# A conditioned residual layer: the order annealed anew, row totals and SBUF low parts on GpSimd, W in two halves

## The chip, the cores and the metric

One NeuronCore of a Trainium2 chip runs the kernel. The metric is the device time of one execution in microseconds, as the median of several runs. The engines are TensorE (PE in the profile, PEld for its weight loads), VectorE (DVE), ScalarE (ACT), GpSimd (POOL) and SyncE (SP, which issues most of the DMAs). Each engine works through its own list of instructions in order, and they wait for each other by semaphores.

## The reference

x is (4, 1024, 512), cond (4, 256), W (1536, 512), b (512), all fp32.

```python
hidden = jnp.concatenate([cond, cond], axis=-1)
x_mean = jnp.mean(x, axis=1, keepdims=True)
fused = jnp.concatenate([x, x_mean * ones_L, hidden[:, None, :] * ones_L], axis=-1)
out = x + jax.nn.relu(jnp.einsum('bld,do->blo', fused, W) + b)
```

So there is one large product, x times the first 512 rows of W, and one bias vector for each of the four rows of the batch: mean(x) times the next 512 rows of W, plus cond times the sum of the last two blocks of 256 rows, plus b.

## The kernel before

The 4096 positions of x are 32 output tiles of 128 positions by 512 columns, eight for each row of the batch. The product is made with fp32r operands split into a high and a low part, hi and lo of x and of W, as hi·hi + lo·hi + hi·lo. With four blocks j of 128 along the 512 summed columns, a tile takes 12 products of 128x128 by 128x512, into one of five PSUM banks (bank t mod 5 for tile t). The last tile is made in two half widths.

x is read twice. Once it comes as z, in rows of 512 bytes, so that a 32x32 block transpose on DVE gives the stationary operand. z comes in ten units (UNITS): tiles 0, 1, 2 to 3, 4 to 7, and then four tiles each; a unit has four transfers `Zu.i` into one of three buffers. The second time it comes as plain x (`Xg.h`, two tiles each) for the residual, into the slot from which the result is stored.

All work is cut into named tasks, and the string ORDER lists them; the loop at the end of the kernel issues them one after the other, so each engine's list is the order of its tasks in the string. A name ends in @d, @a or @p where the engine is chosen there: DVE, ACT or POOL. The tasks:

- `Zu.i`, `Wp.i`, `Mi`, `V`, `C`, `B`, `Xg.h`, `St`: the DMAs of z, of W's first block, of the mean's block, of the condition's block, of cond, of b, of x, and the stores. All are on SP's queue but W0, which is on ACT's. A transfer has one of eight semaphores and is issued when the earlier one with that semaphore has landed.
- `whj`, `wlj` (lines 207, 205, 211): high and low part of W, block j. `fill` (L129): a product of zeros in bf16 that keeps PE going before data is there.
- `Tu.j`, `hu.j`, `lu.j` (L229, L235, L241): for block j of unit u the transpose on DVE, the high part on ACT, which also sums it along the positions into `sums`, and the low part. Of the units of four tiles, the transposes of blocks 0 and 2 go to PSUM (px), those of 1 and 3 to SBUF (xT). GpSimd has no access to PSUM.
- `pt.j.n` (L339): one product; `pt.j`: all three.
- The bias of row r: `ac`, `t`, `g`, `d` make the condition's part, `prr` and `tor.j` (L274 to L281) the means from `sums`, `as` puts the condition's part into a PSUM bank, `mr.j` (L293) adds the mean's four blocks on DVE, `f`, `fa` fold the upper half of the partitions onto the lower, `vh`, `vl` split the result, `pbr` (L317) sums over the partitions and broadcasts with a matmul by ones, and `bc` copies the bias to SBUF. These steps wait for each other, from `to` to `bc`.
- A tile's end, by WAYS. Tiles 0 to 11 (K) are copied out of the bank by ACT before the bias is there (`K`), then `b` on POOL adds the bias (L410), `r` on ACT takes the relu and `F` on POOL adds x (L422). Tiles 12 to 17 (B) are copied with the bias added by DVE (`K`, L414), then `r` and `F` alike. Tiles 18 to 31 (I) get the bias into the bank ahead of the products (`P`, ACT, L393), and `F` on DVE takes relu and sum in one (L397). A bank is free again when `K` or `F` has read it.

Of the kernel before, what the change touches and what calls it, by code (L numbers as in the profile page):

```python
# [18 lines left out]


ORDER = """
W0.0@a W0.2@a W0.1@a W0.3@a Z1.0 Z1.2 Z1.1 Z1.3 Z0.0 Z0.2 Z0.1 Z0.3 W1.0 W1.2 W1.1 W1.3 T1.2 T1.0 T1.1 h1.0
wh0r@d h1.1 l1.0@d wh0l@d l1.1@p Z2.0 Z2.2 Z2.1 Z2.3 T0.1 fill fill fill fill fill fill fill fill fill p1.0.0
T0.0 p1.0.1 h0.1 wl0l@d h0.0 l0.1@d wl0r@d l0.0@p T1.3 p1.0.2 T0.2 h1.3 p0.0.1 W2.0 W2.2 W2.1 W2.3 wh2@d h0.2
p0.0.2 h1.2 p0.0.0 l0.2@p wh1@d p1.2.0 l1.3@p T0.3 wl2@d p1.1.0 h0.3 l1.2@p p0.2.1 p1.1.1 Z3.0 Z3.2 Z3.1 Z3.3
wl1@d p0.2.2 p1.2.2 l0.3@d p0.1.0 p1.1.2 T2.0 p0.1.1 T2.3 p0.1.2 h2.0 T2.2 p1.2.1 B p0.2.0 wh3@a l2.0@d C T2.1
h2.3 p3.0 V wl3@d h2.1 Z4.0 Z4.2 Z4.1 Z4.3 p1.3.0 l2.3@d h2.2 p0.3.0 l2.1@d p0.3.2 pr0 p2.0 l2.2@d M0 M2 M1 M3
p1.3.2 p3.1 p1.3.1 p3.2 K1@a Z5.0 Z5.2 Z5.1 Z5.3 p2.3 T3.1 p0.3.1 T3.0 p2.2 h3.1 p3.3 h3.0 l3.1@d K0@a p2.1
l3.0@d T3.2 p6.1 ac0@p K2@a to0.0 T3.3 p4.0 h3.2 Z6.0 Z6.2 Z6.1 Z6.3 ac1@p h3.3 p7.0 l3.3@d p4.1 t2 t1 p6.0
l3.2@d p7.1 to0.1 t3 t0 g0.0 p4.3 g0.1 d0.0 T4.1 p5.3 T4.0 h4.1 p5.1 T4.2 d0.1 h4.0 p4.2 to0.3 h4.2 l4.0@d  # L30
p5.2 K4@a l4.1@p to0.2 T4.3 p5.0 as0 l4.2@d Z7.0 Z7.2 Z7.1 Z7.3 p6.2 K5@a m0.0 p7.3 g1.0 m0.1 K3@a p6.3 X1.0
d1.0 m0.2 X0.0 g1.1 p7.2 X3.1 h4.3 m0.3 X0.1 p10.0 d1.1 g2.0 l4.3@d p9.2 f0 pr1 d2.0 p9.0 K6@a fa0 g2.1 p9.1
T5.1 K7@a d2.1 T5.3 p10.1 vh0 p8.1 h5.1 vl0 h5.3 p9.3 l5.1@p T5.2 T5.0 p10.2 h5.2 l5.3@p Z8.0 Z8.2 Z8.1 Z8.3
p11.3 h5.0 l5.2@d to1.2 pb0 to1.0 p11.0 l5.0@d bc0@a X4.1 to1.3 p10.3 to1.1 as1 b1@p p11.1 m1.0 K10@a p11.2
K9@a b2@p T6.0 g3.1 T6.1 p8.0 m1.1 h6.1 p15.3 T6.3 r2 l6.1@p p14.3 m1.2 r1 p15.1 K11@a m1.3 b0@p h6.3 p8.3
T6.2 f1 p8.2 l6.3@d Z9.0 Z9.2 Z9.1 Z9.3 b4@p h6.0 p12.1 fa1 T7.1 p12.2 vh1 b3@p l6.0@d h7.1 p12.3 vl1 h6.2
p15.2 F1 T7.3 K8@a p16.1 T7.0 h7.3 l6.2@d b5@p pb1 p16.0 bc1@a pr2 l7.1@d p14.2 h7.0 F2 T7.2 as2 p13.1 to2.0
to2.1 h7.2 m2.0 p13.2 r4 to2.2 p12.0 m2.1 r0 F4 p15.0 to2.3 m2.2 p13.0 F0 m2.3 p14.0 l7.0@d f2 p13.3 l7.3@p
g3.0 S0 fa2 X5.1 p16.3 K12@d vh2 d3.0 p14.1 r3 vl2 p16.2 r12 K14@d b7@p p17.0 K13@d r14 pb2 l7.2@d p17.3 F3
bc2@a T8.0 p17.2 P18 T8.2 P19 p17.1 T8.3 S3 r5 X5.0 T8.1 p18.3 S2 h8.2 F5 X3.0 p18.1 h8.0 l8.2@d X4.0 p18.2  # L40
X2.1 r13 K16@d d3.1 h8.3 p19.2 K15@d h8.1 p19.0 K17@d P21 l8.1@p l8.0@d p18.0 X6.1 as3 pr3 S1 T9.0 p21.2 P20
X2.0 l8.3@p T9.1 h9.0 S4 p21.0 T9.2 r7 p21.3 to3.0 F14 F18 P22 p19.1 h9.2 T9.3 p20.0 h9.1 to3.2 b6@p P23 p19.3
to3.1 m3.0 h9.3 b11@p p22.2 m3.1 p22.0 m3.2 b8@p p23.0 to3.3 m3.3 p20.3 f3 p20.1 r16 fa3 p22.1 F16 l9.2@d vh3
p20.2 r15 vl3 p22.3 b10@p F19 p23.1 F22 S19 pb3 l9.1@p p23.3 X1.1 l9.3@d bc3@a S5 p23.2 r17 F20 S22 b9@p P24
S16 p21.1 S20 P27 p24.1 X6.0 r11 F21 p27.1 F11 l9.0@d P26 p27.2 F23 r6 p27.3 P25 F6 p27.0 p25.2 F7 F27 p26.0
S27 P31r F12 r9 p24.2 S7 S6 P28 p31.2r S11 p31.1r F9 p31.0r p24.3 p26.1 F13 S9 X7.0 p26.2 S18 F15 S12 p25.1
X7.1 p24.0 S13 F17 p26.3 F24 p25.0 F26 S24 P29 p28.1 S26 p25.3 p28.0 F25 p29.0 S25 P30 p28.3 S15 r8 S21 p29.3
P31l F8 S17 r10 p31.1l p28.2 F10 S8 p31.3r S14 F28 p30.3 F31r p30.1 S28 S31r p30.2 S10 p30.0 p29.2 F30 p29.1
S30 p31.3l S23 F29 p31.0l p31.2l S29 F31l S31l
""".split()  # L50


# [1 line left out]
def kernel(  # L54
# [81 lines left out]
    def task(name):  # L136
        def put(f):
            assert name not in tasks, name
            tasks[name] = f
        return put  # L140

    def dma(e, **kw):
        (nc.scalar if e == "a" else nc.sync).dma_start(**kw)  # L143
# [115 lines left out]
    for r in range(B):  # L259
        for k in range(KH):  # L260
            @task(f"g{r}.{k}")
            def _(e, r=r, k=k):
# [8 lines left out]
        @task(f"pr{r}")
        def _(e, r=r, n_early=n_early):
            if n_early > 1:
                nc.vector.tensor_reduce(tot[:, r], sums[:, r, :, :n_early], AX.X, ALU.add)  # L274
# [1 line left out]
            nc.vector.tensor_scalar(pre[:, r], src, 1.0 / L, None, ALU.mult)

        for j in range(J):
            @task(f"to{r}.{j}")
            def _(e, r=r, j=j, n_early=n_early):  # L280
                nc.vector.scalar_tensor_tensor(  # L281
                    tot[:, r, j : j + 1], sums[:, r, j, n_early : n_early + 1], 1.0 / L, pre[:, r, j : j + 1],
                    ALU.mult, ALU.add,
                )
# [4 lines left out]

        for j in range(J):  # L290
            @task(f"m{r}.{j}")
            def _(e, r=r, j=j):
                nc.vector.scalar_tensor_tensor(  # L293
                    acc, w_mean[:, j, :], tot[:, r, j : j + 1], acc, ALU.mult, ALU.add
                )
# [16 lines left out]
        def _(e, low=low, high=high):
            nc.vector.tensor_tensor(v_acc[high], acc[low], v_acc[low].bitcast(F32), ALU.subtract)  # L313

        @task(f"pb{r}")
        def _(e):
            nc.tensor.matmul(acc, lhsT=ones, rhs=v_acc, start=True, stop=True)  # L317

        @task(f"bc{r}")
        def _(e, r=r):  # L320
            nc.scalar.activation(biases[r], acc, AF.Copy)  # L321
# [139 lines left out]
```

## Time and profile before

| | us |
|---|---|
| median of three runs | 113.5 |
| lowest, highest | 112.43, 113.69 |
| the profiled execution | 113.67 |
| its span, first to last instruction | 111.9 |

The page gives, for one execution, the busy time of each engine, then the span in 40 slices, DMA queues, the chain of work that ended last, and groups of like instructions. Three further views of the trace are used: busy time of the engines in chosen stretches (the columns are the stretch, its length, then busy us and instructions of PE, PEld, DVE, ACT and POOL, the granted clock, the DMA share and GB/s), the list of waits (who waited for whom: us in total, times, longest), and the time line (start, length, engine, line, operation, and in brackets how long the engine stood idle before it and for whom).

### The profile page before, as it was taken

How to read it: one execution, taken by the hardware profiler on the slowest of the kernel's cores; microseconds unless marked ns; L12 is line 12 of the kernel's file. 1: busy time of each engine (PE TensorE's matmuls, PEld its weight loads, DVE VectorE, ACT ScalarE, POOL GpSimd, SP SyncE). 2: the span in 40 equal slices, each digit the busy share in tenths (PEclk: the TensorE clock that was granted, in tenths of full speed). 3: DMA queues.
4: the chain of work that ended last, by engine and by line, in shares of the span. 5: the costliest groups of instructions: out<-in, count | busy, mean ns of one | idle time of the engine just before them, and what ended most of it. 6: DMA issues, size and time to landing. Idle time of an engine off the chain costs nothing.

```text
span 111.9 us, 1435 instructions
## 1 busy us (share of the span) xinstructions
PE 97.5 (87%) x409; PEld 75.9 (68%) x409; DVE 81.2 (73%) x150; ACT 61.5 (55%) x152; POOL 65.6 (59%) x59
## 2 busy tenths in 40 slices
...
GB/s 86 172 190 239 217 230 346 212 227 259 242 226 230 227 230 244 373 287 191 244 196 196 205 117 247 408 348 403 75 3 204 405 390 316 282 406 402 405 403 77
DMA packets 27698, 28.41 MB, mean 254 GB/s; under 512 B 1701, under 2 KB 18345, under 8 KB 27690
## 3 DMA queue, kind: packets, MB, share of 16 engines
...
## 4 chain that ended last, share of the span: by engine, by line
PE 34%; DVE 34%; ACT 8%; issue 6%; DMA 6%; SPq 4%; POOL 3%; DVEq 0%; ACTq 0%
PE po L339 34%; DVE acc L293 10%; DVE lo L241 5%; DVE xT L229 5%; DVE tot L281 4%; DVE px L229 4%; SPq L143 4%; DMA out_dram<-x 3%; ACT hi L235 3%; ACT term L263 2%; DMA z<-in_x_dram 2%; DVE v_acc L313 2%; DVE acc L305 2%; ACT fold L301 2%; POOL cond L267 1%
## 5 line engine op out<-in xcount | busy, mean ns | idle before, releaser
L339 PE MATMUL po<-w_hi,hi 128*128 128x512 f32 (+1 forms) x132 | 51.4, 395 | 4.1 <-DVE o L414 2.1
L339 PE MATMUL po<-w_lo,hi 128*128 128x512 f32 (+1 forms) x132 | 51.7, 395 | 1.1 <-DVE w_lo L211 1.1
L339 PE MATMUL po<-w_hi,lo 128*128 128x512 f32 (+1 forms) x132 | 51.4, 391 | 0.0
L339 PEld LDWEIGHTS po<-w_hi,hi 128*128 128x128 f32 x132 | 25.3, 192 | 11.7 <-ACT hi L235 2.6
L339 PEld LDWEIGHTS po<-w_lo,hi 128*128 128x128 f32 x132 | 25.6, 194 | 6.6 <-DVE w_lo L211 1.5
L422 POOL TENSOR_TENSOR x<-o,x 128x512 f32<-128x512 f32 x18 | 22.9, 1290 | 10.1 <-ACT o L418 9.4
L339 PEld LDWEIGHTS po<-w_hi,lo 128*128 128x128 f32 x132 | 25.5, 193 | 4.8
L397 DVE SCALAR_TENSOR_TENSOR x<-po,x 128x512 f32<-128x512 f32 x13 | 8.8, 686 | 13.9 <-PE po L339 13.9
L241 POOL TENSOR_TENSOR lo<-xT,hi 128x512 fp32r<-128x512 f32 (+1 forms) x13 | 13.0, 1011 | 9.6 <-ACT hi L235 9.6
L410 POOL TENSOR_TENSOR o<-o,bias 128x512 f32<-128x512 f32 x12 | 16.2, 1366 | 0.4 <-ACT bias L321 0.4
L235 ACT ACTIVATE hi<-xT 128x512 fp32r<-128x512 f32 (+2 forms) x24 | 12.0, 499 | 7.9 <-DVE xT L229 7.8
L229 DVE STREAM_TRANSPOSE xT<-z 128x512 f32<-128x512 f32 (+2 forms) x24 | 12.2, 529 | 5.6 <-DMA z<-in_x_dram 5.6
L293 DVE SCALAR_TENSOR_TENSOR acc<-w_mean,tot,acc 128x512 f32<-128x512 f32 x16 | 11.9, 747 | 0.4
L393 ACT ACTIVATE po<-bias 128x512 f32<-128x512 f32 x13 | 7.6, 593 | 8.1 <-DVE x L397 8.1
L235 ACT ACTIVATE hi<-px 128x512 fp32r<-128x512 f32 (+1 forms) x16 | 9.0, 563 | 4.4 <-DVE px L229 2.5
L418 ACT ACTIVATE o<-o 128x512 f32<-128x512 f32 x18 | 10.9, 620 | 0.4 <-DVE o L414 0.4
L241 DVE TENSOR_TENSOR lo<-xT,hi 128x512 fp32r<-128x512 f32 (+2 forms) x11 | 9.4, 851 | 2.3 <-ACT hi L235 2.3
L241 DVE TENSOR_TENSOR lo<-px,hi 128x512 fp32r<-128x512 f32 (+1 forms) x16 | 10.3, 641 | 0.6 <-ACT hi L235 0.6
L229 DVE STREAM_TRANSPOSE px<-z 128x512 f32<-128x512 f32 (+1 forms) x16 | 10.4, 667 | 0.0
L406 ACT ACTIVATE o<-po 128x512 f32<-128x512 f32 x12 | 7.0, 588 | 5.0 <-PE po L339 4.9
L257 POOL TENSOR_TENSOR wc<-x 128x512 f32<-128x512 f32 x2 | 2.5, 1282 | 11.6 <-DMA x<-in_L_cond_W_dram 11.6
L267 POOL TENSOR_TENSOR cond<-b_sb,term 128x512 f32<-128x512 f32 x4 | 5.6, 1402 | 4.1 <-ACT term L263 4.1
...
## 6 DMA issues: line engine op xcount, KB each, us to landing
...
```

Source lines behind the costliest of these rows:

```text
L229: nc.vector.transpose(xT.rearrange("p (n t) -> p n t", t=Q), zs[u % Z_BUFS][:, : n * NQ, j * Q : (j + 1) * Q])
L235: nc.scalar.activation(his[buf][:, col : col + m], xT, AF.Copy, accum_out=sums[:, r, j, s : s + 1])
L241: nc_of[e].tensor_tensor(los[buf][:, col : col + m], xT, his[buf][:, col : col + m].bitcast(F32), ALU.subtract)
L267: nc.gpsimd.tensor_tensor(conds[r % 2], conds[r % 2] if k else b_sb, terms[k], ALU.add)
L293: nc.vector.scalar_tensor_tensor(acc, w_mean[:, j, :], tot[:, r, j : j + 1], acc, ALU.mult, ALU.add)
L339: nc.tensor.matmul(v, lhsT=a[:, col : col + P], rhs=m, start=WAYS[t] != "I" and key not in done, stop=done.count(key) == 3 * J - 1, skip_g ...
L393: nc.scalar.activation(bank(t), biases[r], AF.Copy)
L397: nc.vector.scalar_tensor_tensor(x_tile(t), bank(t), 0.0, x_tile(t), ALU.max, ALU.add)
L406: nc.scalar.activation(o, bank(t), AF.Copy)
L410: nc_of[e].tensor_tensor(o, o, biases[r], ALU.add)
L418: nc.scalar.activation(o, o, AF.Relu)
L422: nc.gpsimd.tensor_tensor(x_tile(t), o, x_tile(t), ALU.add)
```

## The change

- ORDER is a new list. Its tasks are those of before but for the points below.
- `l0.1`, `l0.3`, `l3.1`, `l3.3`, `l4.3`, `l6.3`, `l7.1` and `l9.3` go from DVE to POOL and `l1.1` from POOL to DVE, so that from unit 3 on all low parts of SBUF pieces are on POOL and all those of PSUM pieces on DVE.
- `pr` and the four `to` of a row on DVE become one `to` on POOL: two instructions of 128x4 for rows 1 to 3, three for row 0.
- W's first block comes in two groups of four transfers, of two blocks each, and no longer in three groups of one, two and one blocks. `wh0r` and `wh1` are on ACT, `wh3` on DVE.
- There are 11 `fill` in place of 9.
- Eight matmuls stand at the end of the kernel, into the bank `acc`, which nothing reads after them, with 128, 96 or 66 columns of the stationary operand, from column 0 or 1.

The new list is given here up to `pb3` and for its last lines.

```diff
@@ ORDER @@
...
+W0.0@a W0.2@a W0.1@a W0.3@a Z0.0 Z0.2 Z0.1 Z0.3 Z1.0 Z1.2 Z1.1 Z1.3 wh0l@d wh0r@a wh1@a W1.0 W1.2 W1.1 W1.3
+wl0r@d wl0l@d T0.0 T0.1 h0.0 wl1@d h0.1 l0.0@p fill fill fill fill fill fill fill fill fill fill fill p0.0.0
+p0.0.2 Z2.0 Z2.2 Z2.1 Z2.3 p0.1.0 T1.0 l0.1@p T1.1 p0.1.2 h1.0 T0.2 p0.0.1 T0.3 h1.1 p0.1.1 T1.3 p1.0.0 h0.3
+l1.0@d p1.0.2 l1.1@d h1.3 l0.3@p p1.1.0 Z3.0 Z3.2 Z3.1 Z3.3 wh3@d h0.2 p1.0.1 p1.1.2 wh2@d l0.2@p p0.3.1 T1.2
+p0.3.0 wl3@d l1.3@p p0.2.0 h1.2 p0.2.1 l1.2@p p1.3.0 wl2@d p1.3.2 C p1.2.0 T2.2 V p1.1.1 p0.2.2 T2.0 h2.2 B
+p1.2.1 p1.3.1 h2.0 Z4.0 Z4.2 Z4.1 Z4.3 l2.2@d p1.2.2 p0.3.2 T2.3 p2.2 l2.0@d h2.3 p2.0 l2.3@d T2.1 p2.3 h2.1
+l2.1@d p3.0 Z5.0 Z5.2 Z5.1 Z5.3 p3.1 T3.3 p2.1 T3.2 h3.3 t2 p3.2 T3.0 h3.2 l3.3@p p3.3 K1@a l3.2@d h3.0 t3
+ac0@p t1 p6.2 T3.1 K2@a l3.0@d p4.2 M0 M2 M1 M3 h3.1 t0 p4.3 l3.1@p g0.0 p6.0 K0@a K3@a p6.3 ac1@p p6.1 d0.0
+g0.1 p7.0 T4.3 Z6.0 Z6.2 Z6.1 Z6.3 p4.0 T4.1 h4.3 p4.1 T4.0 K6@a l4.3@p T4.2 h4.1 p5.3 h4.2 p7.3 l4.1@p h4.0
+p7.1 K4@a l4.0@d d0.1 p8.3 g1.0 T5.1 p5.2 Z7.0 Z7.2 Z7.1 Z7.3 l4.2@d to0 as0 p5.0 d1.0 T5.3 h5.1 p11.3 T5.2
+p5.1 T5.0 l5.1@p p8.2 h5.0 m0.0 p8.1 g1.1 X5.0 m0.1 g2.0 p9.0 d1.1 Z8.0 Z8.2 Z8.1 Z8.3 m0.2 h5.3 p11.0 h5.2
+m0.3 l5.3@p p9.3 K5@a l5.0@d p11.2 f0 d2.0 g2.1 p8.0 fa0 p9.2 l5.2@d K8@a d2.1 T6.1 p7.2 vh0 p10.1 vl0 X0.0
+K7@a T6.2 p13.3 h6.1 X0.1 T6.3 p10.3 l6.1@p T6.0 pb0 X1.0 p9.1 bc0@a to1 p10.0 as1 b2@p X4.0 K9@a p11.1 m1.0
+g3.0 p13.0 b0@p m1.1 Z9.0 Z9.2 Z9.1 Z9.3 h6.3 p10.2 m1.2 g3.1 b1@p p14.0 h6.0 m1.3 p12.0 l6.0@d f1 l6.3@p
+p12.1 T7.1 K10@a p12.3 K11@a fa1 b5@p p14.1 T7.0 vh1 X4.1 h7.1 p12.2 vl1 b3@p h6.2 p15.0 T7.3 h7.0 l6.2@d pb1
+l7.1@p p14.2 h7.3 T7.2 p16.3 bc1@a l7.0@d h7.2 p13.2 T8.0 as2 to2 p16.2 l7.3@p r0 m2.0 p15.1 r1 m2.1 r2 F0
+p14.3 m2.2 p15.3 F1 m2.3 p15.2 K12@d f2 p13.1 d3.0 S1 fa2 p16.0 X5.1 T8.1 S0 vh2 p17.2 b4@p X3.0 h8.0 vl2
+p17.1 r5 l8.0@d pb2 F2 p16.1 K13@d bc2@a p17.3 T8.3 P18 F5 p17.0 K14@d r3 h8.1 l7.2@d p18.3 P19 K17@d l8.1@p
+p18.2 T8.2 P22 p18.0 T9.0 F3 h8.2 p19.1 r12 l8.2@d p22.3 h9.0 d3.1 T9.1 p22.1 h8.3 T9.2 p18.1 r4 K15@d l8.3@p
+h9.1 p22.2 F18 P20 p19.0 F4 T9.3 P23 p19.3 h9.2 p20.1 S4 K16@d h9.3 S18 p23.1 as3 to3 X2.0 b6@p P21 S2 p23.0
+m3.0 S3 p19.2 m3.1 X2.1 b10@p r6 X3.1 p21.3 m3.2 S5 p20.3 X1.1 l9.3@p m3.3 p23.2 l9.2@d f3 p20.2 b7@p fa3
+p22.0 F19 vh3 b9@p p20.0 vl3 p21.1 F20 F12 pb3 F22 p21.2 S20 bc3@a X6.1 l9.0@d p21.0 b8@p P27 r7 p23.3 P24
...
+P29 S24 p28.2 r15 S17 S11 p30.3 F14 S23 p29.2 S16 F15 p28.0 S14 p30.0 F28 F13 p31.3l S28 p30.2 S31r p29.0 S15
+F30 p29.3 S30 p29.1 S13 p31.0l F29 p31.1l p31.2l S29 F31l S31l
 
 
@@ -104,7 +103,7 @@
     cT = sb("cT", [P, KH, Q])
     sums = sb("sums", [P, B, J, 4])
     tot = sb("tot", [P, B, J])
-    pre = sb("pre", [P, B, J])
+    pre = sb("pre", [P, J, 2])
     one = sb("one", [P, 1])
 
     ps_o = [banks.tile([P, D], F32, name=f"po{i}") for i in range(O_BANKS)]
@@ -163,7 +162,7 @@
             @task(f"Z{u}.{i}")
             def _(e, z=z, r=r, i=i, k0=k0, n=n):
                 dma(e, out=z[i * Q : (i + 1) * Q, : n * NQ], in_=zv[r, i, :, k0 * NQ : (k0 + n) * NQ, :])
-    for part, (j0, n) in enumerate([(0, 1), (1, 2), (3, 1)]):
+    for part, (j0, n) in enumerate([(0, 2), (2, 2)]):
         for i in range(NQ):
             @task(f"W{part}.{i}")
             def _(e, i=i, j0=j0, n=n):
@@ -266,22 +265,14 @@
             def _(e, r=r, k=k):
                 nc.gpsimd.tensor_tensor(conds[r % 2], conds[r % 2] if k else b_sb, terms[k], ALU.add)
 
-        n_early = len(row_units[r]) - 1
-
-        @task(f"pr{r}")
-        def _(e, r=r, n_early=n_early):
-            if n_early > 1:
-                nc.vector.tensor_reduce(tot[:, r], sums[:, r, :, :n_early], AX.X, ALU.add)
-            src = tot[:, r] if n_early > 1 else sums[:, r, :, 0]
-            nc.vector.tensor_scalar(pre[:, r], src, 1.0 / L, None, ALU.mult)
-
-        for j in range(J):
-            @task(f"to{r}.{j}")
-            def _(e, r=r, j=j, n_early=n_early):
-                nc.vector.scalar_tensor_tensor(
-                    tot[:, r, j : j + 1], sums[:, r, j, n_early : n_early + 1], 1.0 / L, pre[:, r, j : j + 1],
-                    ALU.mult, ALU.add,
-                )
+        @task(f"to{r}")
+        def _(e, r=r, n=len(row_units[r])):
+            add, v = nc.gpsimd.tensor_tensor, sums[:, r]
+            if n == 4:
+                add(pre, v[:, :, :2], v[:, :, 2:], ALU.add)
+                v = pre
+            add(tot[:, r], v[:, :, 0], v[:, :, 1], ALU.add)
+            nc.gpsimd.tensor_scalar(tot[:, r], tot[:, r], 1.0 / L, None, ALU.mult)
 
         @task(f"as{r}")
         def _(e, r=r):
@@ -432,6 +423,9 @@
         name, _, engine = name.partition("@")
         tasks.pop(name)(engine)
 
+    for m, c in ((P, 0), (96, 0), (96, 0), (66, 0), (66, 0), (P, 1), (P, 1), (P, 0)):
+        nc.tensor.matmul(acc[:m], lhsT=his[0][:, c : c + m], rhs=w_hi[:, 1], start=True, stop=True)
+
 
 # ---- launch: one core; inputs and outputs as the reference has them ----
 _INS = ["x", "cond_512", "L0_cond_W", "L0_cond_b"]
```

More of the change, by code (lines that the diff above doesn't have):

```diff
@@ L21 @@
 ORDER = """
[L22 to L46, printed above, removed]
@@ L47 @@
-X7.1 p24.0 S13 F17 p26.3 F24 p25.0 F26 S24 P29 p28.1 S26 p25.3 p28.0 F25 p29.0 S25 P30 p28.3 S15 r8 S21 p29.3
-P31l F8 S17 r10 p31.1l p28.2 F10 S8 p31.3r S14 F28 p30.3 F31r p30.1 S28 S31r p30.2 S10 p30.0 p29.2 F30 p29.1
-S30 p31.3l S23 F29 p31.0l p31.2l S29 F31l S31l
+W0.0@a W0.2@a W0.1@a W0.3@a Z0.0 Z0.2 Z0.1 Z0.3 Z1.0 Z1.2 Z1.1 Z1.3 wh0l@d wh0r@a wh1@a W1.0 W1.2 W1.1 W1.3
+wl0r@d wl0l@d T0.0 T0.1 h0.0 wl1@d h0.1 l0.0@p fill fill fill fill fill fill fill fill fill fill fill p0.0.0
+p0.0.2 Z2.0 Z2.2 Z2.1 Z2.3 p0.1.0 T1.0 l0.1@p T1.1 p0.1.2 h1.0 T0.2 p0.0.1 T0.3 h1.1 p0.1.1 T1.3 p1.0.0 h0.3
```

3 lines of the change are left out of this document (added).

## The prediction

> **What bounds the kernel now.** The page comes first, for the whole; then busy time by stage, to find where PE stands still; then the waits and the time line, to find who it waits for; then the groups, for durations.
>
> ```profile
> span 111.9 us, 1435 instructions
> ...
> PE 97.5 (87%) x409; PEld 75.9 (68%) x409; DVE 81.2 (73%) x150; ACT 61.5 (55%) x152; POOL 65.6 (59%) x59
> ...
> GB/s 86 172 190 239 217 230 346 212 227 259 242 226 230 227 230 244 373 287 191 244 196 196 205 117 247 408 348 403 75 3 204 405 390 316 282 406 402 405 403 77
> ```
> ```profile
> 8.00:12.00 4.00, 3.50 (x8) 2.46 (x9) 3.19 (x9) 1.47 (x9) 2.26 (x4) 0.50 0.79 225
> 12.00:16.00 4.00, 4.00 (x14) 3.14 (x13) 3.97 (x13) 2.20 (x9) 0.00 (x0) 0.65 0.98 228
> 36.00:40.00 4.00, 3.34 (x16) 2.45 (x14) 3.97 (x7) 3.63 (x9) 3.22 (x3) 1.00 1.22 229
> 48.00:52.00 4.00, 2.68 (x12) 1.88 (x10) 3.97 (x7) 3.59 (x10) 4.00 (x4) 1.00 1.18 232
> 60.00:64.00 4.00, 1.86 (x8) 1.13 (x7) 3.80 (x7) 2.84 (x5) 3.69 (x4) 1.00 0.76 185
> 80.00:84.00 4.00, 2.81 (x13) 2.00 (x12) 3.60 (x6) 2.97 (x7) 3.13 (x3) 1.00 0.02 6
> ```
> ```profile
> PEld acc L317 <- DVE v_acc L313: 4.8, 4, 1.9
> PE acc L317 <- DVE v_acc L313: 3.3, 3, 1.5
> PE po L339 <- DVE o L414: 2.1, 1, 2.1
> ```
> ```profile
> 57.73 0.39 PE L339 MATMUL po<-w_lo,hi 128*128 128x512 f32 x1
> ...
> 60.45 0.39 PE L339 MATMUL po<-w_lo,hi 128*128 128x512 f32 x1
> 62.98 0.50 PE L339 MATMUL po<-w_hi,hi 128*128 128x512 f32 x1 [2.14 <-DVE o L414]
> ...
> 82.40 0.50 PE L317 MATMUL acc<-v_acc,ones 128*128 128x512 f32 x1 [1.20 <-DVE v_acc L313]
> ...
> 106.68 0.28 PE L339 MATMUL po<-w_lo,hi 128*128 128x256 f32 x1
> 107.00 0.42 DVE L377 SCALAR_TENSOR_TENSOR x<-po,x 128x256 f32<-128x256 f32 x1 [0.38 <-PE po L339]
> ```
>
> From 57.73 to 60.45 PE starts 13 products: 0.227 us each. Nothing makes a product cheaper here, so the end is set by when PE may start and where it stands still. It stands still in four places of the steady part: 0.66 us in 36 to 40, 1.32 in 48 to 52, 2.14 in 60 to 64, 1.19 in 80 to 84. Three of them are a row's bias matmul (`pb`) waiting for `vl` on DVE, the fourth a PSUM bank that `K12` on DVE frees late. In all four stretches DVE is 3.6 to 3.97 of 4 us busy: DVE's queue is the limit up to the last bias. Before 15 us there is a second loss, the clock of 0.50. Behind the last `pb`, at 82.40, PE runs without a stop to 106.68, and the rest of the span, 5.2 us, is the last half tile and its store. DMA is the third resource: about 230 GB/s while z is loaded, and almost nothing at 77 to 84 (75, 3).
>
> **The change, part by part.** Durations:
>
> ```profile
> L241 DVE TENSOR_TENSOR lo<-xT,hi 128x512 fp32r<-128x512 f32 x6 | 7.4, 1236 | 2.3 <-ACT hi L235 2.3
> L241 DVE TENSOR_TENSOR lo<-px,hi 128x512 fp32r<-128x512 f32 x14 | 9.4, 675 | 0.6 <-ACT hi L235 0.6
> L241 POOL TENSOR_TENSOR lo<-xT,hi 128x512 fp32r<-128x512 f32 x8 | 10.3, 1294 | 2.6 <-ACT hi L235 2.6
> L241 POOL TENSOR_TENSOR lo<-xT,hi 128x128 fp32r<-128x128 f32 x5 | 2.7, 558 | 7.0 <-ACT hi L235 7.0
> L281 DVE SCALAR_TENSOR_TENSOR tot<-sums,pre 128x1 f32<-128x1 f32 x16 | 6.1, 403 | 0.0
> L276 DVE TENSOR_SCALAR pre<-sums 128x4 f32<-128x4 f32 x3 | 2.5, 823 | 0.0
> L410 POOL TENSOR_TENSOR o<-o,bias 128x512 f32<-128x512 f32 x12 | 16.2, 1366 | 0.4 <-ACT bias L321 0.4
> L422 POOL TENSOR_TENSOR x<-o,x 128x512 f32<-128x512 f32 x18 | 22.9, 1290 | 10.1 <-ACT o L418 9.4 <-DMA x<-in_x_dram 0.7
> L229 DVE STREAM_TRANSPOSE px<-z 128x512 f32<-128x512 f32 x14 | 9.5, 699 | 0.0
> L235 ACT ACTIVATE hi<-px 128x512 fp32r<-128x512 f32 x14 | 8.2, 589 | 3.0 <-DVE tot L281 1.8 <-DVE px L229 1.1
> L448 POOL MEMSET const-float32-0.0<- 128x1 f32 x1 | 0.1, 98 | 0.2 <-issue 0.2
> ```
>
> *lo.* The six full-size `lo` that DVE took from SBUF go to GpSimd: DVE loses 7.4 us, POOL gains 6 x 1.294 = 7.8. The Trainium skill, GPSIMD Engine Reference, "Engine selection", says that two-input elementwise work is about twice as slow on GpSimd and belongs on VectorE. By that rule DVE would save only 6 x 0.675 = 4.1 us for those 7.8. Here the DVE form cost 1.236, near POOL's 1.294, while the same operation from PSUM (px) took 0.675; so I take 7.4.
>
> *Row totals.* `pr` and 16 `to` leave DVE (2.5 + 6.1 us), nine small POOL instructions come. No row shows a 128x4 operation on POOL: below, 0.098 (a memset); above, 0.558 (128x128). The line through 128x128 and 128x512 gives about 0.32 for 4 columns, so 0.7 us for a `to` of two, between 0.2 and 1.1. In sum DVE goes from 81.2 to about 65, POOL from 65.6 to about 76.
>
> *W in halves.* One group of four transfers less; SP is spared four issues, and 256 KB move ahead of the first product. `wh1` and half of `wh0` go to ACT, `wh3` to DVE: all early, hidden behind arrivals below.
>
> *Fills.* They run before any operand is there; two more at 0.43 end by 5.7 us, before the first product. Zero.
>
> *Eight matmuls at the end.* They write a bank that nobody reads. At 0.227 each they take 1.8 us behind the last product, at the slow clock's 0.43 3.4 us; both end before the 5.2 us of last tile and store. Zero; were a 96- or 66-column form to cost over 0.65 each, it would show.
>
> *The order.* I count the products that stand ahead of a task in the new list (pT.J is 3, pT.J.N 1, a half tile half of that, `pb` 1), 388 in all, and give PE 0.227 for each between the places that an arrival sets. Rows for these:
>
> ```profile
> 3.35 0.32 ACTq L143 DMA_DIRECT2D x<-in_L_cond_W_dram  x1
> 5.62 0.29 DVE L207 CAST w_hi<-x 128x256 fp32r<-128x256 f32 x1 [0.45 <-DMA x<-in_L_cond_W_dram]
> 6.74 0.47 PE L339 MATMUL po<-w_hi,hi 128*128 128x512 f32 x1 [1.88 <-DVE w_hi L207]
> 17.93 0.71 DVE L229 STREAM_TRANSPOSE xT<-z 128x512 f32<-128x512 f32 x1 [1.92 <-DMA z<-in_x_dram]
> 22.69 2.53 POOL L257 TENSOR_TENSOR wc<-x 128x512 f32<-128x512 f32 x2 [11.57 <-DMA x<-in_L_cond_W_dram]
> 27.30:31.20 3.90, 3.90 (x19) 3.21 (x18) 3.45 (x9) 3.55 (x10) 2.67 (x3) 1.00 1.15 238
> 31.20:36.10 4.90, 4.90 (x23) 4.08 (x22) 4.79 (x7) 4.67 (x11) 4.24 (x4) 1.00 1.22 230
> 65.51 1.31 DVE L229 STREAM_TRANSPOSE px<-z 128x512 f32<-128x512 f32 x2
> 73.97 3.80 POOL L410 TENSOR_TENSOR o<-o,bias 128x512 f32<-128x512 f32 x3
> 76.47 2.33 DVE L293 SCALAR_TENSOR_TENSOR acc<-w_mean,tot,acc 128x512 f32<-128x512 f32 x3
> 84.00:108.00 24.00, 22.96 (x113) 19.16 (x111) 9.17 (x14) 7.26 (x15) 14.93 (x12) 1.00 1.01 355
> ```
>
> Start. The last part of W was issued at 3.35 and used at 5.62; twice as large it comes at about 6.0, and the transposes of unit 0 now stand behind `wh0` and `wl0` on DVE, so the first product moves from 6.74 to about 7.8. From then on nothing in the list is late, where before PE halted twice more. The clock costs 0.2 us on each of 8 to 17 products.
>
> Gate 1, unit 4 (84 products ahead). Z3 was there at 17.93; a quarter megabyte of W now moves before it, worth 0 to 1.1 us at 230 GB/s: I take 17.4. V then took 22.69 - 17.93 = 4.8, a z unit of 1.05 MB takes 4.6 at 230 GB/s: Z4 at 26.8. T 0.70, h 0.59, lo on POOL 1.29, handovers 0.1: `p8.3` at 29.5. PE alone would be there at 7.8 + 84 x 0.227 + clock 1.7 to 3.3 = 28.6 to 30.2. So 29.5, and the clock hardly matters.
>
> Gate 2, `pb0` (136). Z5, now ahead of M, at 31.4, M (4.4 at 238) at 35.8, Z6 at 40.4. From the first `m` to `pb` the chain took 82.40 - 76.47 = 5.9 in row 3, where DVE was free for it. `m0.0` waits for M; DVE then does `l5.2` and `T6.1` between `fa0` and `vl0`, 0.65 not covered by `vh0`: 42.35. PE would be there at 29.5 + 52 x 0.227 = 41.3. A wait of 1.05.
>
> Gate 3, `pb1` (173). `T6.1` ends at 41.5, then h6.1, l6.1 on POOL and `to1` (0.6, 1.3, 0.7): 44.2; chain 5.9; `l6.0` and `T7.1` in between, 0.75 uncovered: 50.85. PE: 42.35 + 8.4 = 50.75. Wait 0.1.
>
> Gate 4, `pb2` (210). Behind `vl1` DVE does T7.3, l6.2, T7.2 at 0.65 (1.31 for two): 52.8; h7.2 and its sum 0.8, `to2` 0.7, chain 5.9, 0.1: 60.3. POOL's seven instructions between `to1` and `to2` end at 44.2 + 7 x 1.27 (3.80 for three) = 53.1, in time. PE: 59.25. Wait 1.05. `K12`, which cost 2.14 us before, now stands in this chain's shadow.
>
> Gate 5, `pb3` (283). POOL has twelve full-size instructions from `to2` (54.3) to `to3`: 54.3 + 12 x 1.29 + 0.7 = 70.5, chain and 0.1: 76.5. PE: 60.3 + 73 x 0.227 = 76.85. No wait.
>
> Tail. 105 product units follow `pb3` before and after; they and the end took 111.9 - 82.40 = 29.5. X6.1 now stands behind S20 and feeds `F27`, which frees a bank for the last tile: 0 to 1.5 us, I take 0.4, as it is issued some 4 us before it is due. Span 76.85 + 29.5 + 0.4 = 106.75. Around the profiled span lay 113.67 - 111.9 = 1.8 us (the profiled run is 0.15% above the median of 113.5, which I neglect): 108.5 us, 4.4% less than before.
>
> **The rivals.** *The bias waits stay.* If new work on DVE and POOL makes each `pb` as late as before, only the bank wait of 2.14 goes: 111.5. For it: the chain is 5.9 us long whatever DVE's load, and as little as 28 products (6.4 us) lie between `as2` and `pb2`. Against it: in rows 0 to 2 `m`, `fa`, `vl` stood behind other DVE work that is now gone.
>
> *POOL becomes the bound.* From `as0` to `pb3` it has 32 full-size instructions and three `to`, 43 us, where PE has 44. At the mean of the `b` row, 1.366, instead of 1.27, `to3` comes 3.1 us later and `pb3` at 79.6: 111.3. One wait for a relu of the size seen (9.4 us in 4 times, 2.35) before it: 113.6, no change. Against it: the excess of 1.366 goes with DVE instructions that read SBUF twice, and those leave. The Trainium skill, SBUF — State Buffer, "Who interferes with whom", says just that: a VectorE instruction contends with a GpSimd one that reads SBUF if it has two SBUF inputs, and otherwise not. By that rule POOL would stay at 1.27; the trace agrees for DVE (1.236 against 0.675).
>
> *Slower: SP's queue starves DMA.* Between X3.0 (206) and S4 (252) SP has nothing to issue, and S4 waits for `F4`, the last instruction before `to3` on POOL, until about 70. Then 31 of 33 stores and eight half loads of x are left, 12.05 MB. At the tail's 355 GB/s they end at 104, in time; below 12.05 / (112.9 - 70) = 281 GB/s the run is slower than 114.6. At 255, the middle between that and the 230 of the z loads: 70 + 47.3 + 1.8 = 119. Against it: only z loads ran that slowly, and none are left.
>
> *Better.* No gate binds: 2.6 us less, 105.9, and with Z3 0.6 earlier 105.3.
>
> **How the numbers follow.** The forecast has 0.45, the bias waits 0.15, POOL 0.20 (half of it as fast as 111.3, half no change), starved DMA 0.08, better 0.12. A measurement of this kernel tells about 1% (112.4 and 114.6 here) from no change. Faster: 0.45 + 0.15 + 0.10 + 0.12 = 0.82; same 0.10; slower 0.08. Range 105.4 to 112.6: it leaves out starved DMA and about 0.1 of POOL's slow half.
>
> **What would show it.** DVE busy near 65 and POOL near 76; the first product at 7.8 and then no gap to 28; waits of about 1 us before `pb0` and `pb2`, none before `pb1` and `pb3`; no wait for `o` by PE; `pb3` at 77 and 29.5 us after it. A `pb3` after 79 with POOL full is the second rival, DMA full for 30 us at the end with PE waiting the third. I would be wrong if z came in slower than 230 GB/s, or a `to` on POOL took over a microsecond.

## The result, and the profile after

| | before | changed |
|---|---|---|
| median, us | 112.97 (4 runs, 112.43 to 113.69) | 109.54 (4 runs, 108.5 to 109.86) |
| ratio, 95% interval | 1 | 0.968 (0.958 to 0.977) |
| the profiled execution, its span | 113.67, 111.9 | 109.66, 107.9 |

The change made the kernel about 3.2% faster; 108.5 us, 4.4% less than before, was forecast. Here and below medians are over all executions of a kernel, and ratios leave out those that took over 1.5% longer than its fastest. The page of the changed kernel has these lines on the whole:

```profile
span 107.9 us, 1436 instructions
...
PE 97.9 (91%) x419; PEld 77.1 (71%) x419; DVE 67.3 (62%) x121; ACT 62.0 (57%) x153; POOL 74.8 (69%) x75
...
GB/s 84 186 255 242 167 222 351 249 221 223 231 242 231 221 227 237 226 219 260 387 286 215 258 378 232 21 301 362 343 407 406 374 262 147 178 276 406 403 405 191
```

DVE is down from 81.2 to 67.3 us, POOL up from 65.6 to 74.8. PE's work is as long as before: the gain is standstill that is gone. The stretches of the steady part and of the end show where:

```profile
8.00:12.00 4.00, 2.27 (x5) 1.82 (x6) 3.88 (x15) 3.02 (x16) 1.66 (x4) 1.00 0.65 180
36.00:40.00 4.00, 4.00 (x20) 3.30 (x19) 3.82 (x7) 3.16 (x8) 3.49 (x4) 1.00 1.22 224
48.00:52.00 4.00, 4.00 (x20) 3.30 (x19) 3.89 (x7) 3.92 (x12) 4.00 (x4) 1.00 1.11 278
56.00:60.00 4.00, 3.61 (x16) 2.67 (x16) 3.81 (x7) 2.29 (x5) 4.00 (x5) 1.00 1.22 211
60.00:64.00 4.00, 4.00 (x20) 3.27 (x18) 4.00 (x8) 3.58 (x8) 3.65 (x3) 1.00 1.07 315
80.00:84.00 4.00, 3.46 (x16) 2.53 (x14) 0.72 (x2) 1.13 (x4) 2.80 (x3) 1.00 1.06 408
92.00:96.00 4.00, 3.45 (x16) 2.38 (x14) 1.94 (x4) 3.65 (x8) 1.37 (x2) 1.00 0.73 201
```

PE (the first busy figure) is now 4.00 of 4 in 36 to 40, 48 to 52 and 60 to 64, where it had 3.34, 2.68 and 1.86. DVE is still 3.8 to 4.0 busy there: a full engine is no loss as long as its results come in time. New stops lie behind the last bias matmul, in 80 to 84 and 92 to 96. The time line names the gates and the late transfers (in the changed kernel's lines L142 is every DMA, L308 a `pb`, L330 a product, L388 an `F` on DVE):

```profile
3.78 1.27 ACTq L142 DMA_DIRECT2D x<-in_L_cond_W_dram  x2
9.73 0.79 PE L330 MATMUL po<-w_hi,hi 128*128 128x512 f32 x1 [3.89 <-ACT hi L234]
...
42.23 0.39 PE L308 MATMUL acc<-v_acc,ones 128*128 128x512 f32 x1
50.61 0.39 PE L308 MATMUL acc<-v_acc,ones 128*128 128x512 f32 x1
59.55 0.50 PE L308 MATMUL acc<-v_acc,ones 128*128 128x512 f32 x1 [0.39 <-DVE v_acc L304]
...
76.24 0.39 PE L308 MATMUL acc<-v_acc,ones 128*128 128x512 f32 x1
82.84 0.69 DVE L388 SCALAR_TENSOR_TENSOR x<-po,x 128x512 f32<-128x512 f32 x1 [2.81 <-issue]
83.87 0.62 SPq L142 DMA_DIRECT2D x<-in_x_dram  x1
91.63 0.69 DVE L388 SCALAR_TENSOR_TENSOR x<-po,x 128x512 f32<-128x512 f32 x1 [8.10 <-DMA x<-in_x_dram]
95.91 0.50 PE L330 MATMUL po<-w_hi,hi 128*128 128x512 f32 x1 [0.55 <-ACT po L384]
```

Only `pb2` still waits. At 82.84 and 91.63 DVE's `F27` and `F25` start late, for halves of x: X6.1, whose last part landed at 82.76, and X6.0, at 91.54. PE then waits at 84.00 for the bank that `F27` freed, and at 95.91 for one that ACT fills with a bias (`P29`) behind the work for `F25`'s bank.

Starts in us, from the matmul rows of each trace:

| | first product | pb0 | pb1 | pb2 | pb3 | from pb3 to the end |
|---|---|---|---|---|---|---|
| before | 6.74 | 39.93 | 52.14 | 63.78 | 82.40 | 29.5 |
| forecast | 7.8 | 42.35 | 50.85 | 60.3 | 76.85 | 29.9 |
| changed | 9.73 | 42.23 | 50.61 | 59.55 | 76.24 | 31.7 |

### The profile page after: what moved, and what is told of

The parts are those of the page before. It is cut to its first block, busy times and chain, and to the rows that moved or that the text cites. A ratio compares the mean times of both kernels' runs of the same rounds, so it can differ in the third digit from the quotient of the medians.

```text
span 107.9 us, 1436 instructions
## 1 busy us (share of the span) xinstructions
PE 97.9 (91%) x419; PEld 77.1 (71%) x419; DVE 67.3 (62%) x121; ACT 62.0 (57%) x153; POOL 74.8 (69%) x75
## 4 chain that ended last, share of the span: by engine, by line
DMA 26%; DVE 16%; POOL 15%; ACT 12%; SPq 10%; PE 8%; issue 7%; ACTq 0%; DVEq 0%; POOLq 0%
DMA x<-in_x_dram 13%; SPq L142 10%; DMA w_mean<-in_L_cond_W_dram 8%; POOL x L413 7%; PE po L330 6%; DVE acc L284 5%; ACT hi L234 5%; POOL lo L240 5%; DVE xT L228 3%; DMA z<-in_x_dram 3%; POOL cond L266 2%; DVE w_lo L210 2%; ACT o L409 2%; DMA x<-in_L_cond_W_dram 2%; DVE lo L240 2%
## 5 line engine op out<-in xcount | busy, mean ns | idle before, releaser
L330 PE MATMUL po<-w_hi,hi 128*128 128x512 f32 (+1 forms) x132 | 51.7, 393 | 5.0 <-ACT hi L234 3.9
L330 PE MATMUL po<-w_lo,hi 128*128 128x512 f32 (+1 forms) x132 | 51.1, 388 | 0.0
L330 PE MATMUL po<-w_hi,lo 128*128 128x512 f32 (+1 forms) x132 | 50.7, 387 | 0.0
L330 PEld LDWEIGHTS po<-w_hi,hi 128*128 128x128 f32 x132 | 25.3, 192 | 11.9 <-ACT hi L234 4.8
L240 POOL TENSOR_TENSOR lo<-xT,hi 128x512 fp32r<-128x512 f32 (+1 forms) x20 | 22.2, 1118 | 16.4 <-ACT hi L234 16.4
L330 PEld LDWEIGHTS po<-w_lo,hi 128*128 128x128 f32 x132 | 25.2, 191 | 5.0
L330 PEld LDWEIGHTS po<-w_hi,lo 128*128 128x128 f32 x132 | 25.2, 191 | 5.0
L388 DVE SCALAR_TENSOR_TENSOR x<-po,x 128x512 f32<-128x512 f32 x13 | 8.7, 686 | 16.5 <-DMA x<-in_x_dram 8.1
L401 POOL TENSOR_TENSOR o<-o,bias 128x512 f32<-128x512 f32 x12 | 15.3, 1296 | 0.0
L266 POOL TENSOR_TENSOR cond<-cond,term 128x512 f32<-128x512 f32 x4 | 5.2, 1302 | 1.9 <-ACT term L262 1.9
L262 ACT ACTIVATE term<-wc,cT 128x512 f32<-128x512 f32 x8 | 5.6, 718 | 1.0 <-POOL wc L256 0.9
L128 PE MATMUL acc<-warm 128*128 128x512 bf16 x11 | 4.9, 632 | 1.0 <-DVE one L120 1.0
```

What stands on the lines that cost most here:

```text
L240: nc_of[e].tensor_tensor(los[buf][:, col : col + m], xT, his[buf][:, col : col + m].bitcast(F32), ALU.subtract)
L330: nc.tensor.matmul(v, lhsT=a[:, col : col + P], rhs=m, start=WAYS[t] != "I" and key not in done, stop=done.count(key) == 3 * J - 1, skip_g ...
L388: nc.vector.scalar_tensor_tensor(x_tile(t), bank(t), 0.0, x_tile(t), ALU.max, ALU.add)
L401: nc_of[e].tensor_tensor(o, o, biases[r], ALU.add)
```

## The experiments

Each kernel is the changed one with the edit shown, unless it says otherwise; ratios are to the kernel before, run on the same chip, with 95% intervals. Before had 112.40, 112.77 and 112.44 us in the first three sets and 112.50 beside the last kernel.

### The late end: is it the transfers of x?

The changed kernel again, for the spread of its end, and two orders in which x for the last tiles is fetched early.

> The changed kernel once more, as the measure for the others of this chip: 0.968 of before, about 109.5 us, with the first product near 9.7, the last bias matmul near 76.2 and 31 to 32 us after it.

```diff
-X3.0 h8.0 vl2
+X3.0 X6.0 X3.1 X2.0 X2.1 X1.1 h8.0 vl2
```

> Five half loads of x (X6.0, X3.1, X2.0, X2.1, X1.1) stand directly behind X3.0, where SP has nothing else to issue. Theory, x comes late in the tail: the waits of DVE and POOL for x go, PE does not stop after the last bias matmul, the tail shrinks from 31.7 to 29.5 us or less; 1.5 to 3 us faster than the changed kernel, 106.5 to 108. Rival, the tail is bound by the stores: the same bytes have to go out, within 0.5 us of the changed kernel.

```diff
-X3.0 h8.0 vl2
+X3.0 X6.0 h8.0 vl2
...
-X6.0 r10
+r10
```

> X6.0 alone stands behind X3.0. Theory: DVE's long wait for x (8.1 us) goes and with it the second of PE's two stops in the tail (0.7 to 0.8 us at 95); the first one (0.7 at 83, for X6.1) stays: 0.7 to 1.5 us faster than the changed kernel. Rival (stores bind): no change.

Again: 108.43 us, 0.968 (0.961 to 0.976), span 106.6; its end behind `pb3` took 29.8 us, not the 31 to 32 expected. The first early order had 111.19 (108.66 to 111.45), no ratio; the second 109.33, 0.973 (0.965 to 0.981). Both were misses: neither beat the changed kernel. Three of the four executions of the first, its profiled one among them, took 111.05 to 111.45; the fourth took 108.66, as long as the changed kernel, and has no trace. The trace of a long one shows X6.1 as the half that is late:

```profile
82.74 0.39 SPq L142 DMA_DIRECT2D x<-in_x_dram  x1
86.95 0.69 DVE L388 SCALAR_TENSOR_TENSOR x<-po,x 128x512 f32<-128x512 f32 x1 [5.68 <-DMA x<-in_x_dram]
```

X6.0 goes into the slot that S0 empties, and S0 landed only at 68.93, behind loads of z and x. SP issues in order: the five halves of x that now stood ahead of S2 and S3 waited with it, S3 behind them landed at 82.69, and X6.1, which goes into the slots of S2 and S3, went out at 82.74 where the changed kernel issued it at 77.30. PE stood still 3.57 us at 84.3. In the profiled execution of the second order (110.71 us) X6.1 landed at 85.36, and PE stood still 2.22 us for the same bank. A transfer put early into an in-order queue holds up all behind it for as long as its own slot is occupied. What spared the shortest executions is not known.

So the third set moved the stores too, and put each X only where its slot is free:

```diff
-F3 h8.2 ... S18 p23.1 as3 to3 X2.0 b6@p P21 S2 p23.0 m3.0 S3 p19.2 m3.1 X2.1 b10@p r6 X3.1 p21.3 m3.2 S5 p20.3 X1.1
+F3 S2 S3 X1.1 h8.2 ... S18 X6.0 X6.1 p23.1 as3 to3 b6@p P21 p23.0 m3.0 p19.2 m3.1 b10@p r6 S5 X2.1 p21.3 m3.2 p20.3
...
-S20 bc3@a X6.1 ... S7 r9 p24.2 X6.0 r10
+S20 X2.0 bc3@a ... S7 X3.1 r9 p24.2 r10
```

> The changed kernel with only the place of transfers changed: S2, S3 and X1.1 behind F3 while DMA is idle, X6.0 and X6.1 behind S18, then S5, X2.1, S20, X2.0 and X3.1 behind S7. Theory, the tail loses time because X6.1 must wait for S2 and S3 and then behind other transfers: F27 no longer waits, PE's stop near 83 (0.7 to 0.8) and the one near 95 go, the tail shrinks to 29.5 us or less: 1 to 2 us faster than the changed kernel. Rival, stores bind the end: within 0.5 us.

It took 107.30 us, 0.955 (0.950 to 0.961), span 105.0. Its chain of work that ended last has, for the end:

```profile
60.01 0.50 PE acc L308
60.51 16.34 PE po L330 x72
76.85 0.23 PE acc L308
77.08 24.01 PE po L330 x117
101.09 1.86 PE acc L427 x8
```

and that of the changed kernel:

```profile
83.87 7.67 DMA x<-in_x_dram
...
91.63 0.70 DVE x L388
...
92.36 0.60 ACT po L384
92.96 2.12 ACT o L409 x4
95.07 0.27 ACT po L364
...
95.91 6.51 PE po L330 x33
102.42 1.86 PE acc L427 x8
```

That of the run again has:

```profile
83.49 0.70 DVE x L388
...
84.66 17.47 PE po L330 x87
102.13 1.86 PE acc L427 x8
```

Without the edit the end hangs on late halves of x: in the profile of the result on X6.0, one transfer of 7.67 us, in that of the run again on X6.1 alone, for `F27` at 83.49. With it the end hangs on PE alone, 117 products in a row with no stop. X6.0 and X6.1 landed at 74.94 and 76.33. From `pb3` to the end it took 28.3 us, against 31.7 and, in the run again, 29.8.

### The start

```diff
-wh0l@d wh0r@a wh1@a W1.0 W1.2 W1.1 W1.3 wl0r@d wl0l@d T0.0 T0.1 h0.0 wl1@d h0.1 l0.0@p
+T0.0 T0.1 h0.0 h0.1 wh0l@d wh0r@a wh1@a W1.0 W1.2 W1.1 W1.3 wl0r@d wl0l@d wl1@d l0.0@p
```

> The first transposes and high parts of x stand ahead of the parts of W on DVE and ACT, so the first product starts about 1.4 us sooner, near 8.3. Theory, arrivals set the pace up to the first bias matmul: the gain is used up by a stop of PE before it, which stays at 41.7 to 42.2; time within 0.5 us of the changed kernel. Rival, the start moves everything behind it: 1.4 us faster.

It took 107.90 us, 0.960 (0.952 to 0.968): 1.5 us sooner at the first product (8.43 against 9.96 in the run again on that chip), but only 0.87 at `pb0` and 0.71 at `pb3`, as PE now stood still for 0.6 us at 39.6, for a bank that ACT copies out late. The ratio's interval overlaps the changed kernel's.

Fills: none (the eleven `fill` tasks left out), and thirty in place of eleven.

> The changed kernel without any of the eleven fills. Theory: PE stands idle for 4 us behind them anyway and starts at the slow clock, so nothing changes: within 0.5 us, the first products 0.43 apart as before. Rival, the fills bring the clock up sooner: the slow products number more than ten and the first bias matmul comes 0.5 us or more later.

> Thirty fills, which last to about 9.4 us, close to the first product. The granted clock should be full at the first product, so the first nine products take 0.23 and not 0.43. Theory, arrivals set the pace up to the first bias matmul: it comes at most 0.5 us sooner, time within 0.5 us of the changed kernel. Rival, the start counts: 1.5 to 2 us faster.

108.65 us, 0.971 (0.963 to 0.978) with none; 107.77, 0.961 (0.956 to 0.966) with thirty. With thirty the first products start 0.23 us apart instead of 0.43, and PE gives about half of that back in stops of 0.28 at 32.7 and 0.66 at 39.7; `pb0` came at 42.05, against 42.23 and, in the run again, 42.83. So a PE that comes sooner meets the arrivals and the chains behind them: the second stop is for a bank that `K8` copies out on ACT, which stands behind `f0`, which waits for M through `m0.0` to `m0.3`.

### DVE's relief or the order?

Each half of the change undone by itself: the six low parts back on DVE (`l3.3 l3.1 l4.3 l6.3 l7.1 l9.3`, `@p` to `@d`); the row totals back on DVE, each where POOL's stood (`to2` becomes `pr2 to2.0 to2.1 to2.2 to2.3`, and so on, with the old bodies; in before these five stood apart in the list); and the list, the fills, W's parts and the end of before, with row totals and low parts on POOL (there `to3` stands ahead of `h9.3`, so one of its four sums is an older one).

> The changed kernel with its six full-size low parts of SBUF pieces (l3.1, l3.3, l4.3, l6.3, l7.1, l9.3) on DVE again. Theory, DVE was the limit and its form of this operation costs 1.2 us beside a busy POOL: the two that fall where DVE is full (48 to 54) come ahead of the third bias matmul, the last one ahead of the fourth; PE stops 1.5 to 3 us more there: 110 to 111.5. Rival, they cost DVE 0.68 each: 0.5 to 1.2 us more. Second rival, only the order counts: within 0.5 us of the changed kernel.

> The changed kernel with the row totals on DVE again, all five instructions of a row where the one of POOL stood. Theory: 0.8 + 4 x 0.4 against 0.45 us, ahead of the bias chain of each row, which has no slack in rows 1 and 2: 1 to 2 us for each of rows 1 to 3, 3 to 5 us slower than the changed kernel: 112 to 114. Rival, the totals are hidden: within 0.5 us.

> The kernel before with its own order, fills and W, but the row totals and the same low parts on POOL. Theory, DVE's load was the limit whatever the order: the four stops of PE before the last bias matmul (6 us) shrink to 2 or less, 108 to 110. Rival, the gain is in the order: 111.5 to 113.

Low parts back: 110.44 us, 0.986 (0.977 to 0.995), with waits of 1.29 before `pb1`, 1.0 around `pb2` and 0.46 at `pb3`. Its groups:

```profile
L240 DVE TENSOR_TENSOR lo<-xT,hi 128x512 fp32r<-128x512 f32 x6 | 5.2, 866 | 0.1
L401 POOL TENSOR_TENSOR o<-o,bias 128x512 f32<-128x512 f32 x12 | 16.1, 1367 | 0.0
```

Those of the changed kernel:

```profile
L240 POOL TENSOR_TENSOR lo<-xT,hi 128x512 fp32r<-128x512 f32 x14 | 18.1, 1298 | 7.4 <-ACT hi L234 7.4
L401 POOL TENSOR_TENSOR o<-o,bias 128x512 f32<-128x512 f32 x12 | 15.3, 1296 | 0.0
L275 POOL TENSOR_SCALAR tot<-tot 128x4 f32<-128x4 f32 x4 | 0.9, 224 | 0.3
L274 POOL TENSOR_TENSOR tot<-sums 128x4 f32<-128x4 f32 x3 | 0.6, 203 | 1.3 <-ACT hi L234 1.3
```

Both means hide two kinds. Three of the lines behind them:

```profile
46.13 4.25 POOL L401 TENSOR_TENSOR o<-o,bias 128x512 f32<-128x512 f32 x3
47.55 1.69 DVE L240 TENSOR_TENSOR lo<-xT,hi 128x512 fp32r<-128x512 f32 x1
...
53.02 0.67 DVE L240 TENSOR_TENSOR lo<-xT,hi 128x512 fp32r<-128x512 f32 x1
```

Four of the six low parts began while POOL stood idle and took 0.67 to 0.69 us. `l6.3` took 1.69 and `l9.3` 0.78, each ending 0.55 us after the `b` that was running when it began (48.68 and 74.72). Ten of the twelve `b` took 1.29 to 1.31, and two took 1.74: `b3` and `b7`, which began while those two low parts were at work. In the changed kernel all twelve took 1.28 to 1.30. In before it was the same: low parts from 0.69 to 1.85, two `b` of 1.74.

Row totals back: 119.10 us, 1.065 (1.055 to 1.074), slower than before and far beyond what was expected. Its time line on DVE and PE, and then on POOL for the same stretch:

```profile
74.87 0.64 DVE L276 TENSOR_SCALAR pre<-sums 128x4 f32<-128x4 f32 x1
75.55 4.96 DVE L281 SCALAR_TENSOR_TENSOR tot<-sums,pre 128x1 f32<-128x1 f32 x4
80.42 3.12 DVE L293 SCALAR_TENSOR_TENSOR acc<-w_mean,tot,acc 128x512 f32<-128x512 f32 x4
...
86.29 0.80 PE L317 MATMUL acc<-v_acc,ones 128*128 128x512 f32 x1 [4.56 <-DVE v_acc L313]
...
74.18 2.57 POOL L410 TENSOR_TENSOR o<-o,bias 128x512 f32<-128x512 f32 x2
76.68 1.31 POOL L241 TENSOR_TENSOR lo<-xT,hi 128x512 fp32r<-128x512 f32 x1
77.92 2.56 POOL L410 TENSOR_TENSOR o<-o,bias 128x512 f32<-128x512 f32 x2
80.41 1.32 POOL L422 TENSOR_TENSOR x<-o,x 128x512 f32<-128x512 f32 x1
```

Four instructions with one column each took 4.96 us, 1.24 each: as long as one full-size instruction of POOL. Taken singly they end at 76.77, 78.00, 79.25 and 80.50, each within 0.03 us of the end of a POOL instruction (76.74, 77.99, 79.23, 80.48). At 58.3, where POOL stood idle, the same four took 0.16 each. In before POOL's queue had gaps at some of these places: the sixteen took 0.40 on average there, 0.64 here.

The old order with both moves: 111.57 us (10 runs), 0.995 (0.990 to 1.001), though DVE had 67.2 us of work and POOL 74.2, the loads of the changed kernel. So the rival of the expectation holds: the moves alone gain at most 1%. And the new order needs the moves. What the old order does with POOL:

```profile
53.69 1.29 POOL L240 TENSOR_TENSOR lo<-xT,hi 128x512 fp32r<-128x512 f32 x1
54.95 1.27 POOL L413 TENSOR_TENSOR x<-o,x 128x512 f32<-128x512 f32 x1
56.19 0.19 POOL L274 TENSOR_TENSOR tot<-sums 128x4 f32<-128x4 f32 x1
...
56.73 3.13 DVE L284 SCALAR_TENSOR_TENSOR acc<-w_mean,tot,acc 128x512 f32<-128x512 f32 x4 [3.80 <-POOL tot L275]
...
61.85 0.50 PE L330 MATMUL po<-w_hi,hi 128*128 128x512 f32 x1 [2.88 <-DVE o L405]
62.67 0.43 PE L308 MATMUL acc<-v_acc,ones 128*128 128x512 f32 x1
```

The last sum of row 2 was there at 53.90, but `to2` stands behind `l7.1` and `F2` on POOL; DVE stood idle 3.80 us and then had `K12` in its chain. In the changed kernel POOL waits for the sum instead (0.66 us before `to2`, 0.63 before `to3`). The last kernel mends the old order for rows 2 and 3, with twelve tasks moved:

```diff
-p15.2 F1 T7.3 ... l7.1@p p14.2 h7.0 F2 T7.2 as2 p13.1 h7.2 to2 m2.0 p13.2 r4 p12.0 m2.1 r0 F4 p15.0 m2.2 p13.0 F0
+p15.2 r0 F0 T7.3 ... p12.0 p14.2 h7.0 T7.2 as2 p13.1 h7.2 K12@d to2 m2.0 l7.1@p F2 p13.2 r4 m2.1 F4 p15.0 m2.2 p13.0 F1
...
-p16.3 K12@d vh2 ... p21.3 F14 F18 ... h9.1 b6@p P23 p19.3 to3 m3.0 h9.3 b11@p
+p16.3 vh2 ... p21.3 F18 ... h9.1 P23 p19.3 h9.3 to3 m3.0 b6@p F14 b11@p
```

> The order of before with row totals and low parts on GpSimd, as in the run that kept the old order, and now twelve tasks moved in it: F0 with its relu goes ahead of F1, the four products p12.0 ahead of the sums of row 2, K12 ahead of m2, l7.1 and F2 on GpSimd behind to2, F14 and b6 behind to3, and to3 behind h9.3. (In the run that kept the old order to3 stood ahead of h9.3, so that one of its four sums was an older one; here it reads all four.) Theory, the row totals stand too late in GpSimd's queue: in the trace of the old order DVE stands still 3.80 us before m2, until to2 ends at 56.69, while the last sum of row 2 is there at 53.9, and the bank wait of PE lies in the shadow of that; so to2 ends at 54.4, K12 is out of the chain, pb2 comes at 59.8 in place of 62.67, the bank wait is gone, pb3 comes at 77.5 to 78 and the median falls by 2 to 2.9 us, to 108.7 to 109.6 where before is at 112.7. First rival, only the bank wait matters and the sums follow anyway: K12 early, pb2 at 62, the time 111 or more. Second rival, row 3 takes it back (GpSimd has the same work ahead of to3 in all): pb2 at 59.8, but pb3 at 80 behind a longer wait, the time 111 to 111.6.

It took 110.59 us, 0.983 (0.977 to 0.989). The mechanism came as the theory had it: `to2` at 52.98, `pb2` at 59.41 and `pb3` at 77.97 (62.67 and 80.54 in the old order), the bank wait gone. The time fell by 1.0 us only, under the 2 to 2.9 expected: the profiled executions differ by 2.1, and the span still has 30.4 us behind `pb3`. The place of the row totals in POOL's queue and of the eleven other tasks moved with it, `K12` among them, is thus part of what the order brings, and the rest lies in several smaller places that were not taken apart.

### Both repairs together

The last tiles' x and the start together:

> The same with the first transposes and high parts of x ahead of the parts of W. Theory: another 0.5 to 0.9 us, from the first bias matmul at 42.0 and not 42.5 on; 1.5 to 3 us faster than the changed kernel, 105.5 to 107. Rival: no more than the tail alone.

106.13 us (105.58 to 108.03), 0.945 (0.940 to 0.950): faster than before and than the changed kernel. The interval just meets that of the tail alone (0.950 to 0.961), so what the start adds to it is not shown.

## Why the prediction was right, and where it was not

The reason held: DVE's late results, not PE's work, set the time of before; the wait for `K12`'s bank went, and of those for `vl` only 0.55 us before `pb2` is left. That the time came within 1% of the forecast is partly luck: PE came 1.9 us later than forecast, M's chain was shorter, and the end behind `pb3` differed by 1.9 us between two executions. The parts, in its order:

- *lo.* POOL's price was right (1.298 against 1.294). DVE's saving of 7.4 was the row of before; undone in the new order the six cost 0.866 each, 5.2 in all. The 1.236 weighed there is not the instruction's own price. With POOL idle it takes 0.67 to 0.69, as the form from PSUM does (0.675), and what lies above that is the wait for a POOL instruction that happens to run. The same holds for the `b` row: 1.366 was not a slower POOL but two of twelve at 1.74, so the second rival's 3.1 us, which put that mean on 32 instructions, had no ground. The Trainium skill, SBUF — State Buffer, "Who interferes with whom", says that a VectorE instruction with two SBUF inputs contends with a GpSimd instruction that reads SBUF. The traces agree in both directions: no `b` of the changed kernel took over 1.30 us, with those low parts gone from DVE, and two took 1.74 again as they returned. (The same section also names VectorE's 2-port modes as contending, which the prediction's "otherwise not" passes over.)
- *Row totals.* A `to` of two instructions took about 0.5 us (53.12 to 53.63 for `to2`), not 0.7. The saving was undersized: in this order the sixteen `to` on DVE took not 6.1 us but 9.3, and where POOL is busy each can be a wait in the bias chain, in row 3 all four; PE stood still 4.72 us for them at 81.34.
- *Fills and eight matmuls: zero.* The fills are shown by the two runs. The eight matmuls end at 104.3, ahead of the span's 107.9; no run left them out alone, so their zero rests on that.
- *Start.* This step failed: "the last part of W ... twice as large comes at about 6.0". Two of W's four parts were issued only at 3.78 and 4.73, the last landed at 7.65, and the first product came at 9.73. The trace names the cause: the two take the semaphores of Z0.2 and Z0.3, which had landed at 3.76 and 4.70, 0.02 us before. In before only one part of W waited so, for Z1.2, and was out at 3.35. The prediction carried that issue time over and did not follow the eight semaphores through the new list. It cost little, as the run with the transposes first shows.
- *Gates 1 to 3.* As PE came 1.9 us later than forecast and nine products started 0.43 apart, PE and not the arrivals set the time up to `pb1`: no wait before `pb0`, where 1.05 was forecast. M's chain was done at 41.69 (the end of `vl0`), 0.65 sooner than forecast, and PE came 0.9 later than the 41.3 forecast for it. That 42.35 for `pb0` was so near is luck: the two are about equally late.
- *Gates 4 and 5.* Right in kind: a wait before `pb2` (0.55, not 1.05: the last sum of row 2 came 2.44 us behind `pb1` instead of 2.75, and `to2` took 0.51 instead of 0.7), none before `pb3`.
- *Tail.* The term was mis-sized: 0.4 us for X6.1 and `F27`, which cost PE 0.71 at 83.07 and 0.78 in the run again. All behind `pb3` took 31.7 instead of 29.9 in the profile of the result, but 29.8 in the run again, so the larger part of that miss belongs to the one execution. There PE stood still another 0.72 and 0.11 at 94.97, for `P29`. ACT reaches it behind `P30` and four relus, which had waited for `F25` and X6.0 (91.54). It also needs `F24`, which stood behind `F31r` and X7.1 (93.44) and ended at 95.19; `P29` began at 95.28. So X7.1 was almost as much in the way. The last store went out 1.36 us after its half tile was done, as SP was still busy with stores. In the run again X6.0 was there at 89.92 and neither was seen. What was left out is the queue: SP issued nothing from 59.75 to 69.10 (21 GB/s at 67 to 70), and afterwards every x stood behind stores. This is the place of the third rival, paid mostly in late loads.

Of the rivals, the bias waits did not stay. POOL's queue held up row 2 in the old order with the moves, by the place of `to2` and not by slower instructions as the rival had it, and not in the new order. The sum, 106.75 for the span, lies between the two profiled ones of this kernel (107.9 and 106.6).
